# Two layers on one core: the first layer's last unit is finished inside the second layer's attention, and the second layer's first keys are made beside the first layer's scans

## The chip, the core and the metric

One core of a Trainium2 chip runs the whole program. The number that counts is the device time of one execution in microseconds; the reported one is the median of several runs. The profile is one further execution, recorded by the hardware profiler.

## The reference

The input x has 4 sequences of 1024 tokens with 256 channels, in float32. Two layers follow each other. Each takes six modulation rows per sequence from a small vector (`silu(c) @ wmod`): shift and scale for the norm before attention, a gate for its result, and the same for the feed-forward part. Gates are pushed away from zero.

```
h = layernorm(x) * (1 + ca) + sa;   x = x + ga * attention(h)
h = layernorm(x) * (1 + cb) + sb;   x = x + gb * feed_forward(h)
```

- Layer 1, attention: a linear recurrence. Token-shifted mixes give r, k, v, g and a decay d; per head (16 heads of 16 channels) a 16 x 16 state goes through the tokens: `y_t = r_t (S + u k_t v_t)`, `S = d_t S + k_t v_t`. Then a group norm, a gate and W_o.
- Layer 1, feed-forward: a router picks two of eight experts for a token, in order of tokens and with a capacity (so a unit needs the counts of those before it); every expert is computed for every token and weighted.
- Layer 2, attention: for each pair of tokens (i, j) and each of 64 channels, `e = relu(ssqrt(q_i + k_j))`; scores are `e . Wphi`; their exps weight both the values and `e` itself.
- Layer 2, feed-forward: gated, with three hidden matrices of 1024.

## The kernel before

The order of the instructions on each engine is written out by hand: Python generators are advanced step by step, and each `yield` ends a step.

**Head.** `block_kernel` loads x (four DMAs of 1 MB), then calls `modulation(0)`, which gives `cols` (shift and scale by channel) and `rows` (gates spread over partitions), and then `first_layer`.

**Layer 1, `first_layer`.** The 4096 tokens are eight units of 512. A unit has 32 scan slots (L602, one for each 128 rows of state); a slot is a scan and a product (L604) on DVE, a product k v on POOL (L545), and two copies of a carry on ACT (L594, L600). The v rows are spread over partitions by way of DRAM: `repeat` issues eight DMAs on SP's queue for two slots. After each slot three generators are advanced: `mid` (`projections` of the next unit, 23 steps), `side` (`chained`: `outputs` of the unit before, `route`, its router, and `prologue` of the unit after next, norm and shift), and, in two slots of three, `moe` (`experts`, 16 steps of a unit, eight matmul records each, L492). Before the first slot `prologue(0)`, `projections(0)` and `prologue(1)` are run. After the last slot `chained(8)` runs the outputs and router of unit 7 and then `moe` runs dry. Results go to `x1` in DRAM.

**Between.** `modulation(1)` is run for layer 2. `pair_attention` loads its constants, adds the bias rows (`brow`), runs `prepare(0)` (norm, queries, keys and values of sequence 0, all written to DRAM), and `spread_keys` reads the keys back: tile `kB{g}` (g = 0 to 7) holds row 8 i + g of the keys in partitions 16 i to 16 i + 15, with one DMA for each i, 64 in all.

**Layer 2, `pair_attention`.** There are 128 blocks of 32 queries. A block has eight pairs: `Block.pair` makes two tiles of `relu(q + k)` on ACT or DVE (L957, L959), a square root on ACT (L960), and score matmuls (L964); `top` and `exps` (L974, L983) end the scores; `weigh` (L1008, DVE) uses the same tiles once more. Pairs are made ahead into a ring of 12 buffers (`RING`), `AHEAD` = 12. After each `weigh`, `work(ROOM[p])` advances a list of tasks and then the `stream`: `dense(j)` (feed-forward of 256 tokens, from L870 on, weights through three buffers `fw`), added once its two `finish` tasks are done, and `prepare(b + 1)`, inserted at block 12 of each sequence. A Silu or Gelu of `dense` waits for the next block's exp (`between`, `switch`), since both change ACT's table. After the last block the stream is run dry.

Of the kernel before, what the change touches and what calls it, by code (L numbers as in the profile page):

```python
# [26 lines left out]
FB = 256  # L27
RING = 12
# [9 lines left out]
@with_exitstack  # L38
def block_kernel(ctx: ExitStack, tc: tile.TileContext, a, out):
    nc = tc.nc  # L40
    keep = ctx.enter_context(tc.tile_pool(name="keep", bufs=1))


    kept = ctx.enter_context(tc.tile_pool(name="kept", bufs=1, space=DRAM))
    x1 = kept.tile([B * T, C], F32, tag="x1", name="x1")
    x2 = [kept.tile([FB, C], F32, tag=f"x2_{j}", name=f"x2_{j}") for j in range(B * T // FB)]

    ident = keep.tile([P, P], F32, tag="ident", name="ident")
    nc.scalar.dma_start(ident, a["ident"])
    eps = keep.tile([P, 3], F32, tag="eps", name="eps")  # L50
    for i, v in enumerate((EPS_LN, EPS_GN, EPS_RHO)):
        nc.vector.memset(eps[:, i : i + 1], v)
    eps_ln, eps_gn, eps_rho = (eps[:, i : i + 1] for i in range(3))


    def modulation(layer):
        cols = keep.tile([P, 6, 2, B], F32, tag="mcols", name=f"mcols{layer}")
        rows = keep.tile([P, 2, B, C], F32, tag="mrows", name=f"mrows{layer}")
        with tc.tile_pool(name=f"mod{layer}", bufs=1) as mp, tc.tile_pool(
            name=f"modps{layer}", bufs=2, space=PSUM  # L60
        ) as mps:
            w = mp.tile([P, 2, 6 * C], F32, name="wmod")
            nc.scalar.dma_start(w, a[f"wmod{layer}"].rearrange("(k p) n -> p k n", p=P))
            ct = mp.tile([P, 2, B], F32, name="ct")
            nc.scalar.dma_start(ct, a[f"cT{layer}"].rearrange("(k p) b -> p k b", p=P))
            sct = mp.tile([P, 2, B], F32, name="sct")
            nc.scalar.activation(sct, ct, AF.Silu)
            pc = mps.tile([P, 12, B], F32, name="pc")
            for m in range(12):
                for k in range(2):  # L70
                    nc.tensor.matmul(pc[:, m, :], w[:, k, m * P : (m + 1) * P], sct[:, k, :], start=k == 0, stop=k == 1)
            nc.vector.tensor_copy(cols.rearrange("p s c b -> p (s c) b"), pc)
            for s in (1, 4):
                nc.vector.tensor_scalar_add(cols[:, s], cols[:, s], 1.0)
            cb = mp.tile([P, 2, B, P], F32, name="cb")
            for k in range(2):
                nc.vector.tensor_copy(cb[:, k], sct[:, k, :].unsqueeze(2).to_broadcast([P, B, P]))
            for gi, comp in enumerate((2, 5)):
                for b in range(B):
                    pr = mps.tile([P, C], F32, name="pr")  # L80
                    for k in range(2):
                        nc.tensor.matmul(pr, cb[:, k, b, :], w[:, k, comp * C : (comp + 1) * C], start=k == 0, stop=k == 1)
                    g = mp.tile([P, C], F32, name="g", bufs=2)
                    nc.vector.tensor_copy(g, pr)
                    mag = mp.tile([P, C], F32, name="mag", bufs=2)
                    nc.vector.scalar_tensor_tensor(mag, g, -1.0, g, ALU.mult, ALU.max)
                    nc.vector.tensor_scalar_max(mag, mag, 0.25)
                    sg = mp.tile([P, C], F32, name="sg", bufs=2)
                    nc.vector.tensor_scalar(sg, g, 0.0, 2.0, ALU.is_ge, ALU.mult)
                    nc.vector.scalar_tensor_tensor(rows[:, gi, b, :], sg, -1.0, mag, ALU.add, ALU.mult)  # L90
        return cols, rows

    with tc.tile_pool(name="stream", bufs=1) as xp:

        x = []
        for b in range(B):
            xb = xp.tile([P, TPB, C], F32, tag=f"x{b}", name=f"x{b}")
            nc.sync.dma_start(xb, a["x"][b * T : (b + 1) * T, :].rearrange("(t p) c -> p t c", p=P))
            x.append(xb)

        cols, rows = modulation(0)
        first_layer(tc, a, x, cols, rows, ident, eps_ln, eps_gn, x1)
    cols, rows = modulation(1)
    pair_attention(tc, a, x1, x2, out, cols, rows, ident, eps_rho, eps_ln)


def first_layer(tc, a, x, cols, rows, ident, eps_ln, eps_gn, x1):
# [16 lines left out]
    U = 512  # L124
    UT = U // P
    NU = B * T // U
    NJ = 2 * HN
    with tc.tile_pool(name="fl_w", bufs=1) as wp, tc.tile_pool(name="fl_1", bufs=1) as p1, tc.tile_pool(
# [7 lines left out]
        def load(name, shape, src, queue=nc.scalar):  # L136
# [3 lines left out]

        chan = load("chan", [P, 2, 10], a["chan"].rearrange("(k p) n -> p k n", p=P))
# [3 lines left out]
        wm = {  # L145
            k: load(f"W_{k}", [P, 2, C], a[f"W_{k}"].rearrange("(k p) n -> p k n", p=P)) for k in ("k", "r", "v", "g", "o")
        }
        tdw1 = load("td_w1", [P, 2, 64], a["td_w1"].rearrange("(k p) n -> p k n", p=P))
        tdw2 = load("td_w2", [64, C], a["td_w2"])
        heads = load("heads", [P, P], a["heads"])  # L150
        gather = load("gather", [P, 4, 32], a["gather"].rearrange("p (j m) -> p j m", j=4))
        avg = load("avg", [P, P], a["avg"])
        center = load("center", [P, P], a["center"])
        wr = load("wr", [P, 2, NE], a["w_router"].rearrange("(k p) e -> p k e", p=P), nc.sync)
        wg = load("wg", [P, 2, HID], a["w_gate"].rearrange("(k p) n -> p k n", p=P), nc.sync)
        tri = load("tri", [P, P], a["tri"], nc.sync)
        ones = load("ones", [P, P], a["ones"], nc.sync)
        rank = load("rank", [P, NE], a["rank"], nc.sync)
        rank_b = rank.unsqueeze(1).to_broadcast([P, UT, NE])
        w_down = a["w_down"].rearrange("(k p) n -> p k n", p=P)  # L160
        bonus_w = wp.tile([P, 2, P], F32, tag="bonus_w", name="bonus_w")
        for cc in range(2):
            nc.vector.tensor_scalar_mul(bonus_w[:, cc, :], heads, chan[:, cc, CH_U : CH_U + 1])
        carry = wp.tile([P, NJ], F32, tag="carry", name="carry")
        front, shifted, ready, summed, routed = {}, {}, {}, {}, {}
        seen = [None]
# [3 lines left out]

        def rows_of_x(u):
            return x[u * U // T][:, u * UT % TPB : u * UT % TPB + UT, :]

        def normed(u, first, dest):
# [30 lines left out]

        def prologue(u):

            hT = p2.tile([P, 2, U + 1], F32, tag="hT", name="hT")
            if u * U % T:
                nc.scalar.copy(hT[:, :, 0:1], front[u - 1][:, :, U : U + 1])  # L210
            else:
                nc.gpsimd.memset(hT[:, :, 0:1], 0.0)
            front[u] = hT
            front.pop(u - 1, None)
            h = hT[:, :, 1 : U + 1]
            yield from normed(u, 0, h)
            yield
            xx = p2.tile([P, 2, U], F32, tag="xx", name="xx")
# [8 lines left out]
            for m0, m in ((0, P), (P, 32)):  # L227
# [4 lines left out]
                t5.append(p2.tile([m, U], F32, tag=f"t5_{m}", name=f"t5_{m}"))  # L232
                nc.scalar.activation(t5[-1], ps, AF.Tanh)
                del ps
            shifted[u] = (h, xx, *t5)

        def projections(u):

            h, xx, t5a, t5b = shifted.pop(u)
# [3 lines left out]
            def mix(name, cc):  # L243
                f, ch = index[name]
                lhs, rhs = (w2a[32 * f : 32 * f + 32, :], t5a[32 * f : 32 * f + 32, :]) if f < 4 else (w2b, t5b)
# [3 lines left out]
                def done():  # L249
# [3 lines left out]
                    nc.vector.scalar_tensor_tensor(xi, ps, chan[:, cc, ch : ch + 1], xx[:, cc, :], ALU.add, ALU.mult)  # L253
                    nc.gpsimd.tensor_add(xi, xi, h[:, cc, :])
# [3 lines left out]
            def project(name, m):  # L258
# [5 lines left out]
                def done():  # L264
# [3 lines left out]
                    if name == "v" and m:  # L268
                        out["vd"] = dr.tile([C, U], F32, tag="vd", name="vd")
                        nc.sync.dma_start(out["vd"].rearrange("(k p) t -> p k t", p=P), out["v"])  # L270
                    if name == "r" and m:
# [41 lines left out]

            steps = [(mix, "k", 0), (mix, "k", 1), (mix, "w", 0), (mix, "w", 1), (project, "k", 0), (project, "k", 1)]
# [4 lines left out]
            for f, *args in steps:  # L319
# [8 lines left out]
            ready[u] = out  # L328
# [43 lines left out]
        def wide(t):  # L372
            return t.unsqueeze(2).to_broadcast([P, UT, NE])

        def small(name, shape=(P, UT, NE)):
            return sp.tile(list(shape), F32, tag=name, name=name)

        def largest(src, name):
            top = small(f"{name}_top", (P, UT))
            nc.vector.reduce_max(top, src, axis=AX.X)  # L380
            hit = small(f"{name}_hit")
            nc.vector.tensor_tensor(hit, src, wide(top), ALU.is_equal)
            nc.vector.tensor_mul(hit, hit, rank_b)
            nc.vector.reduce_max(top, hit, axis=AX.X)
            nc.vector.tensor_tensor(hit, hit, wide(top), ALU.is_equal)
            return hit

        def route(u):
# [9 lines left out]
            gates = small("gates")  # L398
            s1 = small("s1", (P, UT))
            nc.vector.reduce_max(s1, lg, axis=AX.X)  # L400
            nc.vector.tensor_sub(gates, lg, wide(s1))
# [148 lines left out]
        for _ in prologue(1):  # L550
            next(first, None)
# [678 lines left out]
```

## Time and profile before

| | |
|---|---|
| time, median of 3 runs | 5648.6 us (5643.17 to 5650.59) |
| profiled execution: time, span | 5644.4 us, 5642.6 us |
| busy share of the span: PE, DVE, ACT, POOL | 82%, 81%, 68%, 9% |
| mean granted clock of PE | 0.876 |
| first scan, last scan (start) | 121.6 us, 1176.1 us |
| first exp of the attention (start) | 1453.8 us |
| DMA | 363.8 MB, mean 64 GB/s |

In the profile times are microseconds from the start of the span; a group row ends with busy time, mean nanoseconds of one, and the idle time before it with what ended most of it. "L602" is line 602 of the kernel before. PEld is the weight load of a matmul; SPq and ACTq are DMA issues by those engines. A float32 matmul appears as two records. A busy PE is not PE at its peak, since ends of matmuls are modelled.

### The profile page before, as it was taken

How to read it: one execution, taken by the hardware profiler on the slowest of the kernel's cores; microseconds unless marked ns; L12 is line 12 of the kernel's file. 1: busy time of each engine (PE TensorE's matmuls, PEld its weight loads, DVE VectorE, ACT ScalarE, POOL GpSimd, SP SyncE). 2: the span in 40 equal slices, each digit the busy share in tenths (PEclk: the TensorE clock that was granted, in tenths of full speed). 3: DMA queues.
4: the chain of work that ended last, by engine and by line, in shares of the span. 5: the costliest groups of instructions: out<-in, count | busy, mean ns of one | idle time of the engine just before them, and what ended most of it. 6: DMA issues, size and time to landing. Idle time of an engine off the chain costs nothing.

```text
span 5642.6 us, 74957 instructions
## 1 busy us (share of the span) xinstructions
PE 4644.4 (82%) x28834; PEld 2741.2 (49%) x28834; DVE 4555.4 (81%) x7953; ACT 3842.2 (68%) x3527; POOL 532.1 (9%) x456
## 2 busy tenths in 40 slices
PE   6788888885568878888887888897878888897888
PEld 2233333333235545555554555564546555564556
DVE  3877777852699788889888888989888889889881
ACT  2322222210898888888888888888888888888860
POOL 1543433410000000000000000000000000000000
PEclk7798988997678989888898898898989989898988
DMA  2333333322001111121111112121111211111123
GB/s 91 90 101 92 94 93 94 106 67 67 27 3 46 59 45 61 48 87 54 49 59 42 57 49 86 49 68 40 61 46 64 86 60 48 49 62 45 57 67 111
DMA packets 217734, 363.79 MB, mean 64 GB/s; under 512 B 71168, under 2 KB 115872, under 8 KB 217376
## 3 DMA queue, kind: packets, MB, share of 16 engines
q1 hardware_dynamic: 213120, 353.73, 20.3%
q10 hardware_dynamic: 4256, 5.26, 0.3%
q8 instruction: 227, 3.72, 0.3%
q14 instruction: 131, 1.07, 0.1%
HBM read 335.80 MB, written 23.07 MB: 64 GB/s over the span
## 4 chain that ended last, share of the span: by engine, by line
PE 29%; DVE 20%; ACT 13%; issue 1%; SPq 1%; DMA 1%; POOL 0%; POOLq 0%; ACTq 0%; DVEq 0%
PE ff_ps L893 13%; DVE s L1008 12%; PE sc L964 7%; ACT s L960 6%; DVE s L959 5%; PE xb L989 4%; PE out_ps L912 2%; ACT s L957 2%; PE ff_ps L870 2%; ACT wide L934 1%; ACT L960 1%; PE o L1040 1%; ACT L983 1%; SPq L802 1%; ACT L934 1%
## 5 line engine op out<-in xcount | busy, mean ns | idle before, releaser
L1008 DVE CUSTOM_DVE_ANT_0 s<-s,xb 128x1024 f32<-128x1024 f32 x2048 | 2411.0, 1214 | 39.0 <-PE xb L989 37.5
L960 ACT ACTIVATE s<-s,eps 128x2048 f32<-128x2048 f32 x1024 | 2039.3, 2001 | 381.4 <-DVE s L959 364.3
L964 PE MATMUL sc<-s,wsel 128*32 128x256 f32 x16384 | 1260.3, 434 | 698.0 <-ACT s L960 696.8
L964 PEld LDWEIGHTS sc<-s,wsel 128*32 128x32 f32 x16384 | 468.1, 118 | 1310.4 <-ACT s L960 914.3
L959 DVE TENSOR_SCALAR s<-kB,qt 128x1024 f32<-128x1024 f32 x1280 | 947.9, 758 | 114.9 <-DMA kB<-kd 93.3
L893 PE MATMUL ff_ps<-wide,fw 128*128 128x256 f32 x4096 | 986.4, 390 | 11.0 <-ACT wide L934 7.2
L957 ACT ACTIVATE s<-kB,qt 128x1024 f32<-128x1024 f32 x768 | 875.2, 1140 | 59.5 <-DVE ew L1008 43.7
L893 PEld LDWEIGHTS ff_ps<-wide,fw 128*128 128x128 f32 x4096 | 769.8, 193 | 187.9 <-issue 76.7
L989 PE MATMUL xb<-ex,pick 128*128 128x256 f32 x2048 | 588.9, 437 | 9.4 <-ACT ex L983 9.1
L989 PEld LDWEIGHTS xb<-ex,pick 128*128 128x128 f32 x2048 | 421.0, 217 | 198.7 <-issue 73.2
L492 PE MATMUL e_ps<-wd,hid 128*128 128x512 f32 x1024 | 478.4, 616 | 1.0 <-DVE acc L475 0.9
L545 POOL TENSOR_TENSOR kv<-vb,out_k 128x512 f32<-128x512 f32 x256 | 324.1, 1274 | 264.1 <-DVE state L602 193.2
L602 DVE TENSOR_TENSOR_SCAN state<-dec,carry,kv 128x512 f32<-128x512 f32 x256 | 325.9, 1273 | 11.1 <-POOL carry L597 8.4
L492 PEld LDWEIGHTS e_ps<-wd,hid 128*128 128x128 f32 x1024 | 198.5, 199 | 276.3 <-issue 270.2
L1056 POOL TENSOR_TENSOR xr<-xr,fin 128x256 f32<-128x256 f32 x32 | 35.3, 1103 | 3108.1 <-DVE fin L1054 3090.0
L870 PE MATMUL ff_ps<-wide,fw 128*128 128x256 f32 x1024 | 258.7, 402 | 2.3 <-DVE wide L857 1.5
L594 ACT COPY carry<-state 128x1 f32<-128x1 f32 x255 | 47.9, 188 | 292.4 <-DVE state L602 291.6
L604 DVE TENSOR_TENSOR pr<-state,rec 128x512 f32<-128x512 f32 x256 | 176.0, 687 | 71.2 <-PE yp L568 24.0
L882 DVE TENSOR_TENSOR wide<-ff_ps,ffn_s 128x512 f32<-128x512 f32 x128 | 87.9, 687 | 179.8 <-PE ff_ps L893 178.8
L870 PEld LDWEIGHTS ff_ps<-wide,fw 128*128 128x128 f32 x1024 | 201.0, 202 | 51.1 <-issue 14.3
L475 DVE SCALAR_TENSOR_TENSOR acc<-e_ps,comb,acc 128x256 f32<-128x256 f32 x224 | 107.0, 478 | 93.1 <-PE e_ps L492 88.5
L1008 DVE DVE_READ_ACCUMULATOR2_ANT ew<- 128x1 f32 x2048 | 167.3, 82 | 0.0
(202 smaller groups left out, 3833.7 us busy)
## 6 DMA issues: line engine op xcount, KB each, us to landing
fw<-in_ffw_dram SPq DMA_DIRECT2D x352, 512.0 KB, 3.3
vb<-vd SPq DMA_DIRECT2D x1024, 64.0 KB, 2.4
wd<-in_w_down_dram SPq DMA_DIRECT2D x32, 1024.0 KB, 5.6
kB<-kd SPq DMA_DIRECT2D x256, 64.0 KB, 2.4
x<-in_x_dram SPq DMA_DIRECT2D x4, 1024.0 KB, 13.7
vd<-out_v SPq DMA_DIRECT2D x8, 512.0 KB, 3.1
x<-x SPq DMA_DIRECT2D x32, 128.0 KB, 1.7
wide<-x SPq DMA_DIRECT2D x8, 512.0 KB, 3.8
```

Source lines behind the costliest of these rows:

```text
L492: nc.tensor.matmul(ps, hid[:, k, t * P : (t + 1) * P], wd[:, k, :], start=k == 0, stop=k == HID // P - 1)
L545: nc.gpsimd.tensor_mul(kv, vb[:, g % 2, :], ready[u]["k"][:, n // HN, :])
L602: nc.vector.tensor_tensor_scan(s[:, 1 : U + 1], dec, kv, c, ALU.mult, ALU.add)
L604: nc.vector.tensor_mul(pr, s[:, 0:U], rec)
L870: nc.tensor.matmul(ps[:, h, :], w[:, k, o : o + P], hT[:, k, :], start=k == 0, stop=k == 1)
L893: nc.tensor.matmul(ps[:, h, :], w[:, k * P : (k + 1) * P], of[:, k, :], start=k == 0, stop=k == 7)
L957: nc.scalar.activation(t[:, h, :], kB[self.b][g], AF.Relu, bias=q)
L959: nc.vector.tensor_scalar(t[:, h, :], kB[self.b][g], q, 0.0, ALU.add, ALU.max)
L960: nc.scalar.activation(t, t, AF.Sqrt, bias=eps_rho)
L964: nc.tensor.matmul(self.sc[32 * j : 32 * j + 32, 0:256], wsel[:, g, 16 * (1 - s) : 16 * (1 - s) + 32], t[:, h, 256 * j : 256 * (j + 1)], s ...
L989: nc.tensor.matmul(xb[:, 256 * j : 256 * (j + 1)], pick[:, j, s, :], self.ex, start=True, stop=True)
L1008: nc.vector.tensor_tensor_reduce(t[:, h, :], t[:, h, :], self.xb[s], 1.0, 0.0, ALU.mult, ALU.add, ew[:, self.n % 4, col : col + 1])
```

## The change

1. **Head.** The first 512 rows of x are loaded alone, the rest later. Weights are issued ahead of the modulation, in the order of use; 12 loads that the first scans don't need are issued on SP after the first v rows. `modulation(layer)` works on four partitions (the four sequences), transposes the columns, and puts the gates into DRAM, from where they are spread. Only 18 of 23 steps of `projections(0)`, in another order (v first), stand before the first slot; `prologue(1)`, `modulation(1)` and `value_row` (the bias row of layer 2) come into unit 0's slots.
2. **Single buffers** for hT, xx and the tanh tiles in layer 1; a prologue waits in the order of emission until the unit before has used them (`free`).
3. **Keys.** In units 6 and 7 `chained` ends with `keys(0)` and `keys(1)`: norm, queries, keys and values of the two halves of sequence 0. In unit 7 `moe` is advanced in every slot.
4. **Key rows.** Keys are written to DRAM 16 times over (`kd` is 8 x 128 x 1024), so a `kB` tile comes with one DMA of 512 KB. In `prepare` the eight writes have a `yield` each.
5. **Unit 7.** After the last scan its y and gate go to DRAM (`yg`). `first_rest`, the first entry of the attention's stream, does its outputs, router and experts (the class `Router` holds the router's steps for both places), with `hid` in one buffer of the ring; until it ends pairs are made 11 ahead instead of 12. `fw` has four buffers.
6. **Constants** of the attention are arranged on the host (`We4`, `Wphi`) and loaded after the keys; w3's scale is multiplied in on POOL.

```diff
+        def keys(u):
+            hT = p1.tile([P, 2, U], F32, tag="wide", name="kT")
+            yield from normed(u, 0, hT, cols_of[1])
...
+            t = p1.tile([P, U], F32, tag="res", name="kn")
+            nc.scalar.copy(t[0:64, :], ps)
+            to = link["kd"].rearrange("g (i r) t -> i g r t", r=16)[:, :, :, u * U : (u + 1) * U]
+            for i in range(8):
+                nc.sync.dma_start(to[i], t[8 * i : 8 * i + 8, :].unsqueeze(1).to_broadcast([8, 16, U]))
...
+                t = p1.tile([P, 2, C], F32, tag="res", name="vn")
+                nc.scalar.copy(t, ps)
...
         def chained(u):
-            if u:
+            if not u:
+                while 0 not in free:
+                    yield
+                yield from prologue(1)
+                yield from modulation(1)
+                yield from value_row()
+            else:
                 yield from outputs(u - 1)
                 yield
                 yield from route(u - 1)
             if u + 2 < NU:
+                while u + 1 not in free:
+                    yield
                 yield from prologue(u + 2)
+            else:
+                yield from keys(u + 2 - NU)
...
-        finished(prologue(0))
-        first = projections(0)
-        for _ in prologue(1):
-            next(first, None)
-        finished(first)
+        head = prologue(0)
+        next(head)
+        finished(modulation(0))
+        finished(head)
+        load_x(0, UT, UT)
...
+        begun = projections(0)
+        for _ in range(18):
+            next(begun)
...
-                if n == NJ - 4:
-                    finished(mid)
+                while n == NJ - 4 and u + 1 < NU and u + 1 not in started:
+                    next(mid, None)
+                    next(side, None)
...
-                if n % 3:
+                if n % 3 or u == NU - 1:
                     next(moe, None)
...
-        for _ in chained(NU):
-            next(moe, None)
+        out = ready.pop(NU - 1)
+        nc.sync.dma_start(link["yg"][:, 0:2, :], out["v"])
+        nc.sync.dma_start(link["yg"][:, 2:4, :], out["g"])
         finished(moe)
...
         def spread_keys(b, g):
-            for i in range(8):
-                nc.sync.dma_start(t[16 * i : 16 * i + 16, :], kds[b][8 * i + g : 8 * i + g + 1, :].to_broadcast([16, T]))
+            nc.sync.dma_start(t, kds[b][g])
...
+        def first_rest():
...
+            for m in range(HID // P + 2):
...
+                elif m:
+                    nc.scalar.activation(hid[:, m - 1, :], ps.pop(m - 1), AF.Silu)
...
+            for i in range(NE // 2):
+                for t in range(UT):
...
+                    for k in range(HID // P):
+                        nc.tensor.matmul(
+                            ps, hid[:, k, t * P : (t + 1) * P], halves[k // 2][:, k % 2, :], start=k == 0, stop=k == HID // P - 1
+                        )
+                    if last is not None:
+                        weighted(*last)
...
+                    yield 6
+                    yield
+                    yield
+            ahead[0] = RING
...
-        for _ in prepare(0):
-            pass
-        values(0)
+        kds[0], vds[0], kB[0] = link["kd"], link["vd"], {}
+        queries(0, link["qd"], nc.scalar)
         for g in range(8):
             spread_keys(0, g)
+        loads()
+        values(0)
...
-        AHEAD = RING
-        tasks, stream = [], []
+        ahead = [RING - 1]
+        tasks, stream = [], [first_rest()]
```

## Prediction

> **What bounds the kernel now.** I read the page's slices first, then the busy times by stage, then the timeline and the queues' issues in the two places where the slices are thin.
>
> ```profile
> PE   6788888885568878888887888897878888897888
> DVE  3877777852699788889888888989888889889881
> ACT  2322222210898888888888888888888888888860
> ```
> One slice is 141 us. Two stages lie behind each other: layer 1 (eight units of scans, slices 1 to 8) and the pair attention (from slice 11). Between them, in slices 9 and 10, no engine is full, and the first slice is half empty. Both gaps are the change's object. By stage (unit boundaries are the first scan of each unit, L602):
>
> ```profile
> 121.00:205.00 84.00, 64.21 (x142) 17.84 (x142) 76.01 (x92) 24.31 (x87) 54.52 (x46) 0.78 0.40 118
> 486.00:633.00 147.00, 129.50 (x342) 51.72 (x341) 114.79 (x181) 38.87 (x112) 57.39 (x49) 0.91 0.34 94
> 930.00:1064.00 134.00, 126.88 (x334) 50.19 (x337) 107.96 (x164) 33.14 (x104) 59.93 (x51) 0.91 0.36 102
> 1064.00:1180.00 116.00, 92.39 (x269) 38.50 (x262) 99.19 (x153) 21.54 (x85) 40.58 (x34) 0.90 0.31 91
> ...
> 1180.00:1224.00 44.00, 38.06 (x96) 17.81 (x95) 24.52 (x41) 4.85 (x8) 5.87 (x6) 0.99 0.18 60
> 1224.00:1247.00 23.00, 16.37 (x46) 8.99 (x47) 6.08 (x29) 7.48 (x12) 0.00 (x0) 0.72 0.15 46
> 1247.00:1304.00 57.00, 54.54 (x128) 23.82 (x126) 17.89 (x40) 0.00 (x0) 2.92 (x4) 1.00 0.13 44
> 1304.00:1337.00 33.00, 21.01 (x80) 18.10 (x80) 12.49 (x44) 0.21 (x1) 0.00 (x0) 0.62 0.15 52
> 1337.00:1354.00 17.00, 1.19 (x2) 0.50 (x2) 4.55 (x17) 0.00 (x0) 1.49 (x4) 0.50 0.50 129
> 1354.00:1402.00 48.00, 28.82 (x104) 21.07 (x104) 8.36 (x29) 10.05 (x18) 0.00 (x0) 0.68 0.28 50
> 1402.00:1437.00 35.00, 5.80 (x48) 1.79 (x48) 3.13 (x5) 9.45 (x6) 0.00 (x0) 0.50 0.57 154
> ```
> Columns: window, length, busy of PE, PEld, DVE, ACT, POOL, granted clock, DMA. Units 0, 3, 6, 7 take 84, 147, 134, 116 us: a scan slot never falls under 2.0 us on DVE (scan 1.27 + product 0.69), and what is emitted beside the scans stretches it. From 1180 to 1437 the work is a chain: experts of unit 6 (44), norm and router of unit 7 (23), experts of unit 7 (57, on PE alone), layer 2's modulation (33), constants (17), first keys (48), key rows (35). The last one is the SP queue's:
>
> ```profile
> 1402.04 32.90 SPq L802 DMA_DIRECT2D kB<-kd  x64
> L959 DVE TENSOR_SCALAR s<-kB,qt 128x1024 f32<-128x1024 f32 x1280 | 947.9, 758 | 114.9 <-DMA kB<-kd 93.3
> ```
> 64 issues of 0.51 us each; the pairs wait for them. In the attention:
>
> ```profile
> 1453.00:1679.00 226.00, 150.73 (x1238) 73.93 (x1242) 209.95 (x364) 211.90 (x152) 1.17 (x1) 0.73 0.01 2
> 1679.00:1924.00 245.00, 204.12 (x1567) 130.23 (x1563) 222.08 (x394) 215.54 (x160) 2.34 (x2) 0.90 0.16 54
> 2710.00:2960.00 250.00, 212.18 (x1597) 137.40 (x1596) 223.67 (x395) 218.74 (x162) 3.85 (x3) 0.90 0.16 52
> ```
> The first eight blocks have no dense work: 226 us, DVE and ACT at 93%, PE at 67%. Eight blocks with one dense take 250. So the room for moved work is on PE, and only a little on DVE and ACT.
>
> **Part 1, head and unit 0 (before: 205.8 us to unit 1's first scan).** Before, the first scan starts at 121.6: modulation 13 to 37, then the weights' DMAs, issued only there, until 49, prologue(0) until 66, projections(0) mixed with prologue(1) until 112, value rows 9. After: x comes as 512 KB, 14 weight issues on ACT's queue (0.48 us each, 7 us) stand ahead of its first activation, so sct is ready near 10.5. Three pieces of two matmuls on 4 columns, each with a PSUM copy (3.4 + 2.5 + 2.5 with the copies: 10 us), 8 small transposes, columns and gates on DVE (0.9 + 2.8): 26. The rest of prologue(0) takes what it took from reciprocal to last tanh, 52.3 to 66.3: 14, so 40. Eighteen of 23 projection steps: before, 13 steps and prologue(1) took 65.6 to 102.2, 37 us; minus prologue(1)'s PE and table loads (about 10), plus the v projection and a mix (5): 32. First scan near 74. The value rows' SP issues (16 of 0.46) now run beside projections. But unit 0 inherits: prologue(1), five projection steps, modulation(1), value_row. DVE sum: 32 slots 63, two prologues 2 x 6.9, 11 mixes of 0.75, 4 bonuses of 0.7, modulation 3.7, the rest 1.6: 93. Stalls: units with a prologue beside scans lose about 15 us to it against 7 of DVE work, twice, and the last projection steps are forced out at slot 28. I take 110. Together 184 (168 to 200): gain 22. The 12 loads put off on SP stand behind the first value rows, 6 us of issue, and need not land before unit 1, over 100 us later; were the next value rows late by all of it, it would be 6 us once; gates and bias rows make SP wait for DVE, with four value groups (8 slots) in hand.
>
> **Part 2, units 1 to 5.** Same instructions; single buffers for hT, xx and t5 hold a prologue back until mix g of the unit before, at slot 18, while it starts after slot 22 anyway, behind outputs and router: they are the cover. Without it each of the five units would wait about one slot, 5 us, 25 in all. I take 0 (within 5).
>
> **Part 3, units 6 and 7: keys.** Each gets a norm (DVE 4.1, ACT 2.3), q, k, v matmuls and four PSUM copies (ACT about 2.4). A prologue in the same slots costs 15 us (147 against 134). Keys lack xx and xm (-3) but have a wait: k and v copies share the one buffer "res", so ACT's v copy waits until 8 key DMAs have read it, and behind it stand the carry copies that the scans' products need. Price by the nearest rows: 8 issues x 0.5 + 3.1 (kd<-wide, 256 KB), minus a slot of 3: 4. [...] No row shows such a shape; I keep 5, nearer the row. So keys cost 12 (8 to 18): unit 6 146. Unit 7 also gets an expert step in every slot instead of two in three: 12 + 5, 133. Loss 29 (20 to 40).
>
> **Part 4, end of scans to the first exp (L983, 1453.9): 273.7 before.** After: nine expert steps of unit 6 ran before the end of the scans instead of eight, leaving 7 at 3.43 us: 25. The last x store needs DVE, POOL and SP: 3. Then 8 key loads on SP, 512 KB each; a 512 KB load lands 3.3 us after issue (fw): 4. Then eight pairs, six with 1.14 + 2.0 on ACT and two with 2.0 (23), and matmuls, maximum, table load, exp: 28. Total 60 (50 to 75). qt's 8 issues are on ACT's queue and fit in the expert tail; the constants follow the keys on SP, 6 us, before the first maximum. The product of gates and w3's scale moves from DVE (1.4 us) to POOL, idle here; the first dense needs it 250 us later. Gain 214.
>
> **Part 5, unit 7's remainder in the first blocks.** DVE: reciprocals 6.7, other norm 4.4, norm 4.1, router 29 x 0.22, expert sums 32 x 0.48, gates 1.7: 39. ACT: 8.4, and since each Silu or Exp among Sqrts costs two table loads (1.28 each), 5 x 2.56 = 13: 21. PE 80 us, on an engine that is idle a third of the time. About 80 slots, 10 blocks. Bounds: 21 if only ACT binds, 60 if DVE and ACT add. A dense is the nearest row: it adds (250 - 219) = 31 us for 16 of DVE and 15 of ACT and hides 85 of PE, so they nearly add. I take 50, nearer the dense's way, less something for Silus that may fall together. The ring of 11 instead of 12 is in that. Dense(0) starts two blocks later; denses already run 75 to 110 us behind their inputs and catch up when further behind (starts 3132, 3356, 3612: seven blocks, then eight), so nothing at the tail, one block (31) at worst. Prepare's eight more slots likewise.
>
> **Part 6, key rows at the three batch changes.** The blocks there are 3 to 9 us longer than their like, behind 64 issues; eight issues remove that: gain 15 (5 to 22). The 512 KB writes, 4 MB a batch, have the 18 blocks from block 12 to the next batch's first pair, 500 us, as their cover; late, they would cost what the key rows cost before, 35 a batch. Four weight buffers instead of three: the tail's chain has no DMA in it (the one load on the chain, 4.6 us at 4439, stands behind key rows), so 0.
>
> **Sum.** 22 - 29 + 214 - 50 + 15 = 172. The profiled execution has span 5642.6 and time 5644.4; the median of the runs is 5648.6. 5648.6 - 172 = 5477.
>
> **Rivals.** (a) The remainder costs what it took alone (1180 to 1304: 124) because every step stalls DVE and ACT in order: 74 more, 5551. For: both at 93%. Against: a dense hides 85 us of PE. (b) It hides but for ACT's tables (21), and unit 0 costs its DVE sum (93): 29 + 17 less, 5431. (c) The change doesn't shorten the seam as it says: keys of unit 7 arrive late, [...] and pairs stay paced by rows as before (35 us): 5512. (d) Slower: a dense is tied to each block's exp (Silu and Gelu wait for it), so it takes whole blocks; pushed to another phase it may take nine instead of eight. One block is 31.3 us of lag, and lag is worked off at the end at 102 us a dense instead of 250: 12.8 us a slip, so from 14 slips of 15 the gain is gone; all 15 give +192 - 172: 5669. Against: the catching up just named.
>
> **How the numbers follow.** Forecast 0.61, (a) 0.13, (b) 0.16, (c) 0.05, (d) 0.05, of which 0.01 with just so many slips that nothing is left. The forecast's own terms give 5435 to 5520; the range reaches to (a) and (b): 5410 to 5555. A measurement tells 0.2%, 11 us, from no change: faster 0.95, same 0.01, slower 0.04.
>
> **What would show it.** First scan near 74, unit 1 near 184, units 6 and 7 at 146 and 133, first exp near 1248, first ten blocks near 32 us instead of 28, no wait for kB above 3 us, last dense starting as late after its input as before. Wrong if unit 0 is over 125, the first exp comes after 1290, or the blocks with the remainder exceed 36.

## The result and the profile after

The changed kernel takes 5618.6 us (median of 5 runs, 5598.1 to 5621.2) against 5648.8 (5 runs beside it): ratio 0.9939, interval 0.9921 to 0.9958. It is faster, but by 30 us where 172 were forecast, and the time lies outside the forecast range of 5410 to 5555. The profiled execution has span 5610.4 us, 32.2 less than before. The page's slices after:

```profile
PE   6789888765778778888896788897888897888888
DVE  5777777656888888889988788888889989898951
ACT  2322222117888888888887888888788888888840
```
The pairs now fill their slices (140 us each) from the tenth on instead of the eleventh, and the first slice is fuller on DVE. But there are new thin places: slices 8 and 9, where units 6 and 7 stand, and at slice 22 a 7 on ACT with a 6 on PE above it. By stage (window, length, busy of PE, PEld, DVE, ACT, POOL, clock, DMA share, GB/s): units 0, 3, 6, 7, the seam, and the first 16 blocks.

```profile
67.00:175.00 108.00, 82.14 (x197) 24.12 (x196) 88.88 (x127) 34.19 (x108) 57.40 (x49) 0.76 0.47 138
456.00:603.00 147.00, 130.29 (x341) 51.77 (x340) 115.26 (x181) 38.85 (x112) 57.36 (x50) 0.90 0.32 94
893.00:1066.00 173.00, 135.24 (x378) 58.49 (x377) 112.62 (x179) 40.02 (x115) 59.82 (x51) 0.86 0.34 95
1066.00:1229.00 163.00, 118.51 (x344) 54.50 (x343) 106.30 (x173) 26.82 (x93) 40.68 (x34) 0.84 0.33 88
1229.00:1307.00 78.00, 35.49 (x185) 13.44 (x183) 17.24 (x39) 23.43 (x15) 8.29 (x13) 0.69 0.62 173
1307.00:1583.00 276.00, 205.56 (x1376) 101.34 (x1376) 235.97 (x435) 228.91 (x175) 4.17 (x3) 0.82 0.04 13
1583.00:1834.00 251.00, 208.40 (x1560) 127.47 (x1559) 226.92 (x404) 218.66 (x162) 6.42 (x6) 0.90 0.15 50
```
Unit 3 is what it was. Unit 6 has less DVE work than unit 3 (112.6 against 115.3) and lasts 26 us longer: it waits. The table cuts the spans at the first scan of each unit and at the exps; plus is gained. The last column is one of the two fastest kernels of the experiments (keys on 128 partitions, no yields), 5489.9 us.

Four words stand for stretches from here on. The seam runs from the last scan's product to the first exp. A block is the time from one block's exp to the next one's. The tail is what follows the last exp. The lag of a dense is the number of blocks from the end of its own eight blocks to its first matmul.

| step | forecast, us | measured, us | fastest kernel, us |
|---|---|---|---|
| head and unit 0 | +22 | +30.5 | +33.1 |
| units 1 to 5 | 0 | +6.6 | +6.7 |
| units 6 and 7 | -29 | -86.6 | -41.4 |
| seam (end of scans to first exp) | +214 | +196.1 | +213.8 |
| first 16 blocks | -50 | -56.4 | -54.3 |
| the other blocks | +15 | -14.2 | +7.2 |
| tail (after the last exp) | 0 | -43.7 | -2.1 |
| sum | +172 | +32.2 | +162.9 |

The first large miss, in the timeline of unit 6 (start, length, engine, line, operation, idle before it and what ended it) and the busy time beside it:

```profile
1023.67 19.68 SPq L632 DMA_DIRECT2D kd<-kn  x8
1025.45 0.69 DVE L779 TENSOR_TENSOR pr<-state,rec 128x512 f32<-128x512 f32 x1
1050.46 0.59 ACT L644 COPY vn<-v_ps 128x512 f32<-128x512 f32 x1 [26.64 <-DMA vb<-vd]
1051.26 0.69 DVE L779 TENSOR_TENSOR pr<-state,rec 128x512 f32<-128x512 f32 x1 [22.41 <-ACT state L775]
...
1210.52 0.59 ACT L644 COPY vn<-v_ps 128x512 f32<-128x512 f32 x1 [26.22 <-DMA kd<-kn]
...
1026.00:1042.00 16.00, 3.20 (x14) 2.28 (x12) 2.30 (x4) 0.00 (x0) 1.96 (x2) 0.69 0.48 88
```
The eight key-row writes hold SP for 19.7 us where 4 were reckoned. ACT's value copy cannot overwrite the shared buffer until they have read it, and DVE's product stands still for 22.4 us behind ACT. In unit 6 the trace names the value-row loads (`vb<-vd`), which came last, as what ended ACT's wait; in unit 7, the line at 1210.52, it names the key-row writes for a wait of 26.2 us. The first experiment tells which it is. While the writes run, the DMA share is 0.48 and 88 GB/s move. The preparation of a batch in the attention, SP's queue:

```profile
1963.50 17.92 SPq L955 DMA_DIRECT2D kd<-wide  x6
1981.46 3.94 SPq L1390 DMA_DIRECT2D xr<-x  x1
1985.44 7.54 SPq L955 DMA_DIRECT2D kd<-wide  x2
1993.03 25.69 SPq L980 DMA_DIRECT2D qt<-qd  x8
2019.76 14.38 SPq L973 DMA_DIRECT2D vd<-wide  x4
...
ACT wide L971 <- DMA vd<-wide: 28.0, 1, 28.0
```
Writes, queries and values occupy SP for 70 us; in the kernel before, the eight query loads alone took 6.5 us there. Two blocks at this place take 44 and 48 us, at the next two preparations 43 and 60, 43 and 46, where a usual block takes 31. The kernel before has one block of 43 at each preparation as well (at the first, one of 40 behind it); the second, over 45, is new. In these second blocks ACT waits 14.5, 28.0 (the last line above) and 14.2 us in the value copies: their one buffer is freed by a value write that stands on SP behind the queries and the key rows. And the seam:

```profile
1252.77 12.86 SPq L987 DMA_DIRECT2D kB<-kd  x8
1255.13 18.86 ACTq L980 DMA_DIRECT2D qt<-qd  x8
1281.84 1.15 ACT L1313 ACTIVATE s<-kB,qt 128x1024 f32<-128x1024 f32 x1 [59.14 <-DMA wk<-in_Wk_dram]
```
Keys and queries are issued together from two queues, and the first pair begins 29 us after the first key load. The releaser named (wk) came last by the trace alone; the pair needs kB and qt.

### The profile page after: what moved, and what is told of

The parts are those of the page before. It is cut to its first block, busy times and chain, and to the rows that moved or that the text cites. A ratio compares the mean times of both kernels' runs of the same rounds, so it can differ in the third digit from the quotient of the medians.

```text
span 5610.4 us, 74442 instructions
## 1 busy us (share of the span) xinstructions
PE 4574.4 (82%) x28714; PEld 2695.6 (48%) x28714; DVE 4532.2 (81%) x7889; ACT 3854.0 (69%) x3550; POOL 534.3 (10%) x463
## 4 chain that ended last, share of the span: by engine, by line
PE 44%; DVE 31%; ACT 16%; SPq 4%; issue 3%; DMA 2%; POOL 0%; ACTq 0%; DVEq 0%; POOLq 0%
PE ff_ps L1249 14%; DVE s L1364 13%; PE sc L1320 8%; ACT s L1316 7%; DVE s L1315 5%; PE e_ps L591 5%; PE xb L1345 4%; DVE state L777 2%; ACT s L1313 2%; PE ff_ps L1226 2%; PE out_ps L1268 2%; ACT wide L1290 2%; ACT L1316 2%; DVE pr L779 2%; SPq L955 1%
## 5 line engine op out<-in xcount | busy, mean ns | idle before, releaser
L1320 PE MATMUL sc<-s,wsel 128*32 128x256 f32 x16384 | 1235.4, 427 | 727.2 <-ACT s L1316 725.8
L1249 PEld LDWEIGHTS ff_ps<-wide,fw 128*128 128x128 f32 x4096 | 769.2, 193 | 181.9 <-issue 74.5
L591 PE MATMUL e_ps<-wd,hid 128*128 128x512 f32 x896 | 424.7, 621 | 0.0
L591 PEld LDWEIGHTS e_ps<-wd,hid 128*128 128x128 f32 x896 | 174.8, 201 | 245.0 <-issue 238.4
L1226 PEld LDWEIGHTS ff_ps<-wide,fw 128*128 128x128 f32 x1024 | 200.2, 201 | 50.1 <-issue 12.1
L1330 DVE TENSOR_REDUCE own<-sc 128x1 f32<-128x256 f32 x128 | 54.0, 422 | 170.6 <-PE sc L1320 170.6
```

The costliest lines, as they stand in the source:

```text
L591: nc.tensor.matmul(ps, hid[:, k, t * P : (t + 1) * P], wd[:, k, :], start=k == 0, stop=k == HID // P - 1)
L1226: nc.tensor.matmul(ps[:, h, :], w[:, k, o : o + P], hT[:, k, :], start=k == 0, stop=k == 1)
L1249: nc.tensor.matmul(ps[:, h, :], w[:, k * P : (k + 1) * P], of[:, k, :], start=k == 0, stop=k == 7)
L1320: nc.tensor.matmul(self.sc[32 * j : 32 * j + 32, 0:256], wsel[:, g, 16 * (1 - s) : 16 * (1 - s) + 32], t[:, h, 256 * j : 256 * (j + 1)], s ...
```

## Experiments

Each is the changed kernel with the edit shown or named; ratios, with a 95% interval behind them, are to the kernel before on the same chip. Where several edits are named together, the lines show what differs from the kernel that has the others. Spans, blocks, tails and lags are those of the profiled execution, which can lie some 15 us off the median.

**A buffer of its own for the value copy.**

```diff
-                t = p1.tile([P, 2, C], F32, tag="res", name="vn")
+                t = p2.tile([P, 2, U], F32, tag="xi", name="vn")[:, 0, :].rearrange(...)
```


> The v copies of the keys in units 6 and 7 get a buffer of their own (tag xi, free by then) instead of the one that the key-row writes read. If the shared buffer is the cause of the two stalled slots (33 and 27 us), units 6 and 7 fall from 172 and 164 to about 146 and 138 us and the time by about 50 us. If the SP queue, which the eight writes hold for 20 us, is the cause, the value rows behind it come late instead and the units stay above 160. The attention's stalls in the prepares stay either way.

5590.7 us, 0.9892 (0.9877 to 0.9907). The writes hold SP as long, the copy no longer waits for them:

```profile
1028.60 19.72 SPq L632 DMA_DIRECT2D kd<-kn  x8
1034.22 0.59 ACT L644 COPY vn<-v_ps 128x512 f32<-128x512 f32 x1 [5.47 <-PE v_ps L641]
...
1058.33 2.48 POOL L709 TENSOR_TENSOR kv<-vb,out_k 128x512 f32<-128x512 f32 x2 [11.57 <-DMA vb<-vd]
1066.64 5.99 PE L591 MATMUL e_ps<-wd,hid 128*128 128x512 f32 x8 [11.95 <-DMA wd<-in_w_down_dram]
```
Unit 6 falls from 172.3 to 145.6, what was forecast; unit 7 only from 162.9 to 155.5. So the shared buffer made ACT wait. But the queue has a share too: the writes end at 1048, and unit 7 begins at 1047. What stands on SP behind them is late there: POOL waits 11.6 and then 9.0 us for value rows, PE 12.0 us for an expert's weights. How much of unit 7's remaining excess this makes was not tried apart.

**One key-row write instead of eight** (64 partitions in one DMA, in units 6 and 7, shown here, and likewise in prepare; the columns of Wk are put in another order for it; the eight yields stay).

```diff
-            for i in range(8):
-                nc.sync.dma_start(to[i], t[8 * i : 8 * i + 8, :].unsqueeze(1).to_broadcast([8, 16, U]))
+            nc.sync.dma_start(to, t[0:64, :].unsqueeze(1).to_broadcast([64, 16, U]))
```


> The columns of Wk are put in another order on the host, so that one DMA from 64 partitions writes all key rows [...] instead of eight DMAs from 8 partitions each; buffers and the eight yields stay. If the shape of the writes is the cause: DMA share near 1 in place of 0.5 while they run, 4 MB in under 20 us instead of 55, stalled slots in units 6 and 7 under 12 us (40 us gained), the three stalls of the prepares (16, 30, 15 us) gone: together 80 to 100 us less. If writes to DRAM are slow in any shape, or the shared buffer alone counts, under 30 us less.

5542.0 us, 0.981 (0.9795 to 0.9825): 77 us of the missing 142.

```profile
1025.00 0.56 SPq L631 DMA_DIRECT2D kd<-kn  x1
1037.67 0.59 ACT L643 COPY vn<-v_ps 128x512 f32<-128x512 f32 x1 [12.51 <-DMA kd<-kn]
...
1029.00:1031.00 2.00, 1.53 (x8) 1.00 (x6) 1.18 (x1) 0.00 (x0) 0.74 (x1) 1.00 0.99 197
```
The DMA share is 0.99, at 197 GB/s; units 6 and 7 take 155.3 and 149.4, and the second long block of each preparation falls to 32 us. The write's shape is the largest cost.

**Without unit 7's remainder.** The kernel leaves out unit 7's outputs, router and experts, copies x in their place, and makes pairs 12 ahead from the start.

```diff
-        ahead = [RING - 1]
-        tasks, stream = [], [first_rest()]
+        ahead = [RING]
+        tasks, stream = [], []
+        nc.sync.dma_start(src[NU - 1], a["x"][(NU - 1) * U :, :])
```


> Unit 7's outputs, router and experts are left out (x is copied in place of its result), and pairs are made 12 ahead from the start. The forecast's price for the remainder is 50 us in the first blocks: then the first 16 blocks fall from 527 to near 471 us. For the tail, 43 us longer than before, two theories: if the late dense goes back to the remainder, the tail after the last exp falls from 223 to 180 us and the time by about 100; if it goes back to the longer prepares, the tail stays near 223 and the time falls by about 56.

5569.0 us, 0.9857 (0.9843 to 0.9872). The first 16 blocks fall from 527 to 468 us; before, they took 471. So the remainder costs 59 us there and 50 in the time, where 50 was forecast. The lag of the denses at the end is 8.2 blocks with and without it: the remainder is not its cause.

**First queries ahead of the first keys, on SP.**

```diff
-        queries(0, link["qd"], nc.scalar)
+        queries(0, link["qd"], nc.sync)
```


> The eight query loads of sequence 0 go on SP's queue ahead of the eight key loads instead of on ACT's queue beside them. If the two queues get in each other's way at the seam (the query issues took 18.9 us there against 6 before), the first relu comes about 12 us earlier; if the 4 MB of keys alone fill the DMA engines, nothing changes (within 3 us).

5597.9 us, 0.9905 (0.9889 to 0.9922).

```profile
1261.78 4.41 SPq L980 DMA_DIRECT2D qt<-qd  x7
1266.29 4.21 SPq L987 DMA_DIRECT2D kB<-kd  x8
1270.84 1.15 ACT L1313 ACTIVATE s<-kB,qt 128x1024 f32<-128x1024 f32 x1 [39.01 <-DMA kB<-kd]
```
The same sixteen loads take 9 us of issue one behind the other, and the seam is 60.5 us, the forecast's 60. Side by side they took 21, from 1252.8 to 1274.0.

**Own buffer, one write, queries first, and no yields in prepare.**

```diff
             nc.sync.dma_start(to, kn.unsqueeze(1).to_broadcast([64, 16, T]))
-            for i in range(8):
-                yield
```


> All three mends together: own buffer for the v copies, one 64-partition write of the key rows, query loads ahead of the key loads; and the eight yields that the eight writes had in a prepare go. If the parts add up: unit 6 near 146, unit 7 near 145, seam 60 (78.6 before), no block over 45 us, and 5618 - 28 (buffer, less what the writes share with it) - 61 (row writes in the attention) - 18 (seam), near 5515. If the eight yields are what makes the denses lag (8 blocks at the end against 4), the tail falls from 225 to 180 as well: near 5475.

5533.8 us, 0.98 (0.9784 to 0.9817). The lag at the end is 4.2 blocks and the tail 181.9 us, as in the kernel before (179.8); but the blocks take 4097 us in all against 4033 with one write alone, and one block after each preparation takes 53 to 56 us.

**One write and no yields, nothing else.**

> As the kernel with one row write (5542), but without the eight yields of a prepare. If they make the denses late: lag of the last full dense 4 to 5 blocks in place of 8.2, tail 180 in place of 229, time near 5495. If a prepare costs its three blocks of the stream anyway, lag and tail stay, 5542 within 8.

5571.0 us, 0.9868 (0.9853 to 0.9882): tail 181.9, blocks 4106. The yields do cause the lag and the long tail, and taking them out alone loses 29 us against the kernel with one write.

**The three mends with the yields.**

> The changed kernel with three edits together: key rows in one write over 64 partitions, a buffer of its own for ACT's value copy in units 6 and 7, and the first queries ahead of the first keys on SP; the eight yields in each batch's preparation stay. Theory (the eight-partition writes, the shared buffer and the queries' place are separate costs that add): from 5542 (one write alone) minus about 8 in unit 7 and 4 in unit 6 and minus 18 in the seam, some 5512; unit 6 near 152, unit 7 near 142, first exp near 1250, the tail still 223 to 229 because the yields stay. Rival (the costs overlap, the seam's gain is taken back by the first blocks): 5530 to 5542.

5507.6 us, 0.9747 (0.9726 to 0.9767): seam 60.9, units 148.7 and 140.5, tail 223.3, blocks 4024. Of the 125 us that the three mends gave alone, 111 are there together. The tail stays long, and the blocks are 73 us shorter than without the yields; this profiled execution was 16 us below the median, so some of the 73 may be its own.

**Four key-row writes, from 16 partitions each.**

> Key rows by four writes from 16 partitions each, instead of one from 64; yields and buffers as in the kernel with one write. [...] If only their number counted in the eight-partition writes, this is like one write: packets of 2 KB near 165 ns, time 5542 within 8. If reading from few neighbouring partitions is slow too, packets stay near 312 ns with 16 engines, and the time lies between, near 5565.

"Their number" is that of the DMA engines at work. By share and rate, 2 KB take one of the 16 engines an estimated 165 ns in the one write (0.99, 197 GB/s) and 315 early in the changed kernel's first preparation (0.49, 51 GB/s, 1976 to 1982). 5550.5 us, 0.9837 (0.9819 to 0.9854), 8 us above one write, DMA share 0.77 to 0.94 at up to 179 GB/s. This moved the engines and the partitions together and so did not tell which counts.

**Eight writes of eight partitions, every fourth instead of eight in a row** (likewise in prepare; the columns of Wk are put in an order that fits, and the rows land in DRAM where they did).

```diff
-                nc.sync.dma_start(to[i], t[8 * i : 8 * i + 8, :].unsqueeze(1).to_broadcast([8, 16, U]))
+                o = 32 * (i // 4) + i % 4
+                nc.sync.dma_start(to[i], t[o : o + 29 : 4, :].unsqueeze(1).to_broadcast([8, 16, U]))
```


> The changed kernel with its eight key-row writes each, from 8 partitions as before, but every fourth partition instead of eight in a row (the columns of Wk are put in another order for it). [...] the eight writes of 2 MB hold SP for about 11 us instead of 19.7, and ACT's value copy waits 12 to 14 instead of 26.6; time 5545 to 5570. Rival[...]: DMA share stays at 0.5, SP is held for 18 us or more, time 5605 to 5625.

5539.7 us, 0.9808 (0.9792 to 0.9824), as good as one write. SP is held 8.4 us, ACT's value copy waits 12.1, and in the windows beside the writes of unit 6 and of the first preparation:

```profile
1024.12 8.42 SPq L633 DMA_DIRECT2D kd<-kn  x8
...
1027.00:1032.00 5.00, 2.65 (x13) 2.00 (x11) 2.16 (x3) 0.00 (x0) 1.41 (x2) 1.00 0.53 203
...
1938.00:1943.00 5.00, 2.62 (x19) 1.59 (x20) 4.96 (x10) 4.95 (x5) 0.00 (x0) 0.76 0.51 209
```
The DMA share is still half (0.53 against 0.48 in unit 6), and yet 203 GB/s move instead of 88. The half share is not what made the writes slow; which partitions they read is.

**Keys on 128 partitions** (the three mends with the yields; each column of Wk twice, every partition read 8 times).

```diff
-            nc.sync.dma_start(to, t[0:64, :].unsqueeze(1).to_broadcast([64, 16, U]))
+            nc.sync.dma_start(to, t.unsqueeze(1).to_broadcast([P, 8, U]))
```


> The kernel of the three mends with the yields kept, but the keys' projection fills 128 partitions (each of its 64 columns twice) and the one key-row write reads each partition 8 times instead of 16. Theory ([...] the one write ran at 197 GB/s with all engines busy while loads into 128 partitions ran at 409): the 2 MB write ends in 5 to 6 us instead of 10.6, at 350 GB/s or more; the preparations' 4 MB in 11 instead of 21; time 5480 to 5500. Rival (writes to DRAM are bound at some 200 GB/s whatever the source): the window beside the write stays at 190 to 205 GB/s, time 5503 to 5512.

5492.2 us, 0.9731 (0.9717 to 0.9746). In unit 6 and in the first preparation:

```profile
1029.00:1031.00 2.00, 1.39 (x7) 0.88 (x5) 1.03 (x1) 0.52 (x2) 0.89 (x1) 1.00 1.04 380
...
1908.00:1914.00 6.00, 4.15 (x23) 2.90 (x24) 3.53 (x6) 5.94 (x6) 0.00 (x0) 0.75 1.02 399
```
The rate nearly doubles, from the one write's 197 GB/s to 380, at about the same share of the engines (0.99 and 1.04), so 197 was not the bound of these writes to DRAM. The interval overlaps with that of the kernel it builds on, so the time gained is not settled.

**What the yields part.** Three kernels ask for the cause of the 53 to 56 us blocks. In the first, the values stand ahead of the key rows in prepare; in the next two, the query loads do, without and with the yields.

> The three edits, no yields, and in each batch's preparation the value copies and their writes stand ahead of the key-row write and the queries. Theory (the blocks of 53 to 56 us that came when the yields went are ACT waiting in the value copies, whose one buffer is freed by a write that stands on SP behind the key-row write and the queries): those blocks fall to 42 to 45, the tail stays at 182, pairs sum near 4040 instead of 4097, time 5470 to 5485. Rival (those blocks are ACT waiting for something else, such as the key copies behind PE): they stay over 50 and the time stays within 10 of 5534. A second rival: queries and keys now come too late for the next batch's first pair, which then shows as a stall for kB at the batch change, 20 us or more each.

> The three edits, no yields, and in each batch's preparation the queries' eight loads stand on SP before the key-row write instead of behind it. Theory (with the yields gone, the 53 to 60 us blocks are DVE's norm of the next dense waiting 25 to 32 us for its input, whose load stands on SP behind query loads that take 25 us because 4 MB of key rows run ahead of them): the eight query loads take 6 us on SP as in the kernel before, the long blocks at 20, 53 and 85 fall to 35 or less, the tail stays at 182, time 5455 to 5480. Rival (the key-row write itself holds up any load behind it, so the value writes or the dense's input are late all the same): long blocks over 45, time 5510 to 5535.

> The same place for the query loads, with the eight yields kept. Theory: the yields' only use was to part the dense's input from the queries on SP, so here they bring only the lag of 8.2 blocks and the tail of 223: time about 5500, some 35 above the kernel without them. Rival (the yields also spread PE and ACT work and pay for their lag): equal to or below the kernel without them.

5543.8, 5506.4 and 5505.3 us (0.9812, 0.9756, 0.975). The order of the value copies was the wrong guess: those blocks grew to 59 and 60 us. With the queries first and no yields they are 50, where 35 or less was expected; with the yields none is over 45, but the tail is 229, and the time is the same. The waits in the first of the 50 us blocks:

```profile
DVE ln_st L889 <- DMA wide<-x: 21.6, 1, 21.6
...
ACT wide L968 <- DMA vd<-wide: 16.3, 2, 15.9
```
DVE waits in a dense's norm for the dense's input, which stands on SP behind the value writes, and those land late behind 4 MB of key rows. The next kernel puts those key rows on POOL's queue, in two pieces:

> As the kernel with the query loads before the key-row write and no yields, but in each batch's preparation the key rows are written from POOL's queue in two pieces of 32 partitions; SP carries the rest as before. Theory (the 50 us blocks are SP's queue: value writes and the next dense's input stand there behind 4 MB of key rows): the value writes land in 2 to 4 us instead of up to 20, the blocks at 20, 53 and 85 fall to 35 or less, the tail stays at 182, time about 5506 minus 3 times 15, 5455 to 5470. Rival (the 16 DMA engines are full for 15 to 20 us whichever queue feeds them): those blocks stay at 45 to 52 and the time at 5495 to 5515.

5513.3 us (0.9772), blocks of 46 to 53, and the waits for input and values are still 16.4 and 15.0 us. So most of it is not SP's queue but the transfer itself. The last kernel shortens it (128 partitions, queries first, no yields):

> Keys on 128 partitions with one write, the value copy's own buffer, all queries ahead of the keys, and no yields. Theory (the 50 us blocks after each preparation, which stayed when the write went to POOL's queue, are transfers that wait while 4 MB of key rows fill the engines; from 128 partitions that takes 11 us instead of 21): those blocks fall by about 10 us each to 38 to 42, the tail stays at 182, time 5506 minus 30 minus 5 in units 6 and 7, 5465 to 5480. Rival (those blocks are the preparation's own work, all put in one block when the yields go): they stay at 47 to 51, time 5490 to 5505, the same as with the yields.

5489.9 us, 0.9727 (0.9711 to 0.9743). The blocks are 40 to 42, and the waits:

```profile
DVE ln_st L889 <- DMA wide<-x: 12.0, 1, 12.0
...
ACT wide L968 <- DMA vd<-wide: 7.1, 2, 6.8
```
They shrink by nine to ten us, as was expected of a transfer twice as fast. The time falls by 16 us where 26 to 41 were expected, and equals that of the kernel with the yields and the keys on 128 partitions: here blocks 4056 and tail 182, there 4034 and 223.

**A wider stream** (own buffer, one write, queries first, no yields; more slots for the dense stream in each pair).

```diff
-ROOM = (3, 5, 6, 6, 6, 3, 2, 6)
-LATE = 2
+ROOM = (4, 6, 6, 6, 6, 4, 4, 6)
+LATE = 1
```


> The three mends, and a stream that gets more of each block (ROOM 40 units a block in place of 37, LATE 1 in place of 2). If the denses' lag comes from whole blocks that they take, eight where seven would do, the lag works itself off: tail near 120 to 150 in place of that of the kernel with the three mends, 30 to 60 us less than it. If matmuls that come in larger heaps delay the blocks' own scores instead, blocks grow by 0.3 us or more each and the time by up to 40.

5773.2 us, 1.0226 (1.0211 to 1.0241). The lag falls to 1.7 blocks and the tail to 144.4, but the blocks sum to 4379 instead of 4097, 2.2 us more each, and the time is 239 us above the kernel without the wider stream, where 40 was the worst expected; why blocks grow so much was not followed. A shorter tail is no gain by itself.

## Why the prediction was wrong in size

By the profile 140 of the 172 us are missing: 58 in units 6 and 7, 44 in the tail, 29 in the other blocks, 18 in the seam, 6 in the first 16 blocks; the head and units 1 to 5 gave 15 more than forecast.

**Right.** The head: first scan at 67.4 (forecast 74), unit 1 at 175 (184). Units 1 to 5: their 6.6 us are luck, since two kernels with the same code there (own buffer; queries first) show 0.6 and 0.1. The remainder: 56 us in the first blocks for 50. The key rows at the batch changes: pairs wait 0.6 us for `kB` in all. The seam's mechanism, and its 60 us once the queries came first. With the writes, the buffer, the queries and the yields changed, the time is 5490, 13 us above the forecast of 5477. Of the rivals, (a) and (b) have the remainder at 124 or 21 and are out; (d) saw the lag but not its price; (c) is wrong in the place: the seam's delay came from the queries, and the writes' cost (DMA share 0.48, 88 GB/s) fell into the units and the preparations.

**The step that failed: the price of the key-row writes**, "I keep 5, nearer the row". The row, 256 KB in 3.1 us, was a write from 64 partitions; the new one reads 8 partitions in a row, 16 times over. Eight of them held SP 19.7 us and ACT 26. The 5 was the author's estimate; no row of the kernel before had shown such a shape. By the runs, what decides is which partitions a write reads: 88 GB/s with eight in a row, 203 and 209 with every fourth, both at about half a DMA share; 197 from 0 to 63 and 380 to 399 from all 128, both at a share near 1. Why the rate goes by the partitions was not shown. The 88 is a mean over unit 6, where it starts at 57 and ends above 100. The first preparation of the changed kernel shows it more clearly (early and late in the writes, at about one DMA share):

```profile
1970.00:1976.00 6.00, 5.35 (x40) 2.53 (x39) 3.80 (x7) 5.92 (x5) 0.00 (x0) 0.64 0.49 58
1994.00:2000.00 6.00, 6.00 (x51) 3.93 (x50) 4.56 (x10) 5.49 (x5) 0.00 (x0) 1.00 0.50 141
```
For the first 18 us 50 to 58 GB/s move; then up to 141. Why the rate rises was not tried apart. The four writes from 16 in a row ran at 149 to 179.

The cost came up twice: in units 6 and 7 (58 us more than forecast) and in the preparations, where part 6 gave 500 us of cover to the writes' landing but none to what is queued behind them: the value writes, for which ACT waited 14 to 28 us each time.

**The seam** missed 18 us in one term: the queries' loads "are on ACT's queue and fit in the expert tail". They were issued only with the keys, and held them up.

**The tail.** That "denses already run 75 to 110 us behind their inputs and catch up when further behind", so that the tail stays, and "Prepare's eight more slots likewise": this step fell too. Without the eight yields a preparation sets the denses back by two blocks, and they come back to a lag of 4.2, as in the kernel before. With the yields it is three: the lag goes from 4.2 to 7.2 and stays there, goes on to 10.2, and comes back to 8.2 and no further. Why it stops there was not followed; that the yields cause it is shown by the kernels with one write, with and without them (tail 229 and 182). But the 44 us are not lost whole: with 128 partitions the kernels with and without them end 2 us apart, and the blocks are 22 us shorter with them (52 in the pair with the queries first). Blocks and tail should have been one term; what of the 44 is moved work and what is loss was not parted for the changed kernel itself.

**A sum in part 3** doesn't come out. Its terms, 15 for a prologue, less 3, and 5 for the wait, make 17 and not 12, and 147 less 134 is 13 and not 15. With 15 to 17 the two units would have been forecast to lose 35 to 39 us instead of 29. The fastest kernel loses 41 there, so little is left to explain once the writes are fast.

**Open.** Why unit 7 takes 9 us more than forecast in the fastest kernel and unit 6 only 2 was not followed.

## What to carry to other kernels

Before a DMA is priced by the nearest row, compare the partitions that it reads with that row's: here the same 2 MB ran at 88, 203 or 380 GB/s with eight in a row, every fourth, or all 128. Ask then who shares its buffer and what stands behind it on its queue, and give one buffer more where an engine in the chain must wait for the read. Where a stream runs beside timed blocks, sum the blocks and the tail together, because work that is late in the one is missing in the other.

## What the runs showed that was not expected

The DMA share hides a slow write: at 0.5 the engines moved 88 GB/s or 203, by the partitions read alone; at 1.0 they moved 197 from 64 partitions, 380 to 399 from 128. And small loads from a second queue were not free for large ones here: eight query loads of 32 KB beside eight key loads of 512 KB took 18.9 and 12.9 us of issue, one behind the other on one queue 4.4 (seven of them) and 4.2.
